# Fillers issued by another engine, a longer ring of pages, and other rules for the first pages in a two-layer graph network with experts

## The chip, the cores and the metric

The kernel runs on one core of one Trainium2 chip, all in float32 (bfloat16 only for exact small counts). The core has TensorE (PE: matrix products, with PEld for its weight loads), VectorE (DVE), ScalarE (ACT), GpSimd (POOL) and SyncE (SP, which here only issues transfers). The metric is the device time of one execution in microseconds; the median of three runs counts.

## The reference

8192 tokens (128 graphs of 64 nodes) of 256 values go through two layers. Each layer is a graph network followed by a mixture of experts:

```python
# layer 0
x = x + gnn0(layernorm(x), adj)        # adj @ x, 256 -> 1024, RMS norm, silu, 1024 -> 256
h = layernorm(x)
logits = h @ gate_w.T                  # 64 experts
top_logits, indices = top_k(logits, 6)
scores = softmax(top_logits)
y = sum over the six of scores[k] * (h @ lattice_weights[indices[k]])   # 256 x 256 each
x = x + layernorm(h + y @ out_w.T + out_b)
# layer 1
x = x + relu(adj @ ln(x) @ W_rel + ln(x) @ W_root)
x = x + sum over the best 2 of 8 experts of w[k] * (relu(f @ W1[e] + b1[e]) @ W2[e] + b2[e])   # f = layernorm(x)
```

The result depends on which experts each token chooses, so the kernel sorts tokens by expert while it runs.

## The kernel before

**Four stages.** (1) From 0 to about 584 us, 32 blocks of 256 tokens go through layer 0's graph network and its gate. For each token and each of its six experts POOL scatters a row of 258 values (256 values, the answer's place, the weight) with an indirect store into the table `r0x` in DRAM (`send`, L419, 12 stores of 128 rows per block). DVE keeps the books that give every row its place. (2) From 622 to 1097.6 us the experts work on *pages* of 128 rows. (3) From 1097.6 to about 1450 us layer 0's output and layer 1's graph network run, again 32 blocks; POOL scatters rows for layer 1's experts into `r1x`. (4) The rest is layer 1's experts, bound by PE's products.

**The expert stage.** Pages go in pairs. For each, SP loads two pages from `r0x` into a buffer `px` (`fetch(j)` in the kernel, `Router.fetch` at L652; 129 KB a page), PE transposes them (`flip`, L1159), ACT copies the transposes from PSUM to `pxT` (L1162), PE multiplies them by the experts' matrices, which all lie in SBUF (`apply`, L1188, eight products per pair), DVE scales the products by the weights back into `px` (L1192), and POOL scatters each page's rows to their tokens' places in `r0y` (`reply`, L426). `px` has 22 buffers of one pair each: the fetch of pair j + 22 waits until the replies of pair j have left its buffer. After 188 pairs of full or nearly full pages come 28 half pages (L649). Twelve *early* pages, one for each of the first twelve experts, are done ahead of the page table.

**Order of the work.** PE, DVE and ACT run in the order in which the kernel's loops issue their instructions (`staggered`: fetch stands twelve pairs ahead of apply, flip three). The order on SP and POOL is chosen by the framework's scheduler. A transfer issued by SP or ACT uses one of eight completion semaphores in turn, shared by both engines; it waits until the one before it on that semaphore is complete. POOL's transfers have eight of their own.

**Fillers.** The last page of an expert is not full. For each of the 64 experts a page of filler rows is stored behind its rows in `r0x` before any page that could read it: `fill_end(e)` reads four ends at a time into registers and issues the store (`fill`, L234). It is called in `apply(j)` for j below 64, on ACT's queue. Full pages have no filler rows; their fetches don't wait for the stores. ACT also loads six small vectors beside pairs 8 to 13 (`load_vectors`).

**Rounds and the first blocks.** The page table lists first up to R full pages of each expert (R is the number after the name `"r0"` in `Router(...)`), then the rest, then pages that are not full. The answers of the first R x 64 listed pages are told apart from the later ones (`"last"`, L432). In stage 3 `load_y(b)` loads the answers of block b; for b below READY it needs no later answer. `look_back`, called after block READY - 1, notes how far each expert's rows had come by then; if they don't fit the first pages, a slow branch waits for everything. `fold(b)`, from the eighth block on, adds two of the six answers on DVE before PE sums the others.

**Adjacency.** Each block of layers 0 and 1 uses one of four tiles (`load_adjacency`) of 128 x 2 x 128 values, of which only the diagonal 64 x 64 blocks are loaded; the rest was cleared once, at the start.

Of the kernel before, what the change touches and what calls it, by code (L numbers as in the profile page):

```python
# [19 lines left out]
P = 128  # L20
# [86 lines left out]
class Router:  # L107
# [502 lines left out]
                                       op0=ALU.add, op1=ALU.max)  # L610
        v.tensor_copy(self.total_pages, most)

    def fill_end(self, e):

        if e % 4 == 0:
            _, self.ends = self.nc.values_load_multi_w_load_instructions(
                self.last[0:1, e:e + 4], engines=[ENG.Activation], min_val=0, max_val=self.spare - self.pg,
                skip_runtime_bounds_check_because="the rows of an expert end in its chunk")
        self.fill(self.nc.scalar, self.ends[e % 4])

    def load(self, what, i, engine):

# [44 lines left out]
def two_layer_gnn_moe_kernel(ctx: ExitStack, tc: tile.TileContext, a: dict, out: bass.AP):  # L667
# [13 lines left out]
    K0 = 6  # L681
    E1, F1, _ = a["L1_ffn_W2"].shape
    EARLY = 12
    READY = 6
    FIRST = 4
    FOLD = 2
    LOOK = 20
# [49 lines left out]


    adjacency = []
    for i in range(4):  # L740
        at = const.tile([P, T, P], F32, name=f"at{i}")
        nc.gpsimd.memset(at, 0.0)
        adjacency.append(at)

    def load_adjacency(b):
        at = adjacency[b % 4]
        for g in range(2):
            nc.sync.dma_start(out=at[g * G:(g + 1) * G, :, g * G:(g + 1) * G],
                              in_=adjT[2 * b * T + g:2 * (b + 1) * T:2].rearrange("t m n -> m t n"))
        return at  # L750
# [24 lines left out]
    with tc.tile_pool(name="c0", bufs=1) as c0, \  # L775
            tc.tile_pool(name="work0", bufs=2) as work, \
            tc.tile_pool(name="ph0", bufs=4, space=PSUM) as ph_pool, \
            tc.tile_pool(name="ps0", bufs=2, space=PSUM) as psum, \
            tc.tile_pool(name="pm0", bufs=1, space=PSUM) as pmix:
        mean = c0.tile([P, P], F32, name="mean")  # L780
        nc.gpsimd.memset(mean, 1.0 / H0)
        route = pmix.tile([P, 2, T, E0], F32, name="route")
# [191 lines left out]
        aggregate(0)  # L974
        rest = lambda f: lambda b: f(b) if b else None

        r0 = Router(tc, const, small, dram, N, D, E0, K0, T, P, 14 * P, 4, "r0", 3, ((K0 * N // P - EARLY) // 4 * 4 + 4, E0 // 2 - 4), True)
        r1 = Router(tc, const, small, dram, N, D, E1, 2, T, 2 * P, N, 4, "r1", 1,
                    (N // P // 2 - E1 // 2, E1 // 4, E1 - 1), True, total=out, like=r0)
        assert W == r0.W  # L980
# [135 lines left out]
    with tc.tile_pool(name="wx0", bufs=3, reuse_waits="tile") as wx, \  # L1116
            tc.tile_pool(name="pt1", bufs=4, space=PSUM, reuse_waits="tile") as pt_pool, \
            tc.tile_pool(name="py1", bufs=4, space=PSUM, reuse_waits="tile") as py_pool:
        npair = (r0.pages + 1) // 2
        pairs = [dict(n=min(2, r0.pages - 2 * j), parts=1) for j in range(npair)]  # L1120
        pairs += [dict(n=2, parts=2) for j in range(E0 // 4)]
        regs = {}
        ring = [wx.tile([P, KD, C], F32, name="pxT", bufs=5)]
        over = dict(ln_g=r0.map.rearrange("p j e -> p (j e)")[:, :D], ln_b=r0.nth.rearrange("p j e -> p (j e)")[:, :D],
                    gamma=r0.end[:, :KD], beta=r0.delta[:, :KD], bg=r0.alloc[:, :E1], gbias=r0.none[:, :E1])

        def load_vectors(j):

            if 8 <= j < 14:
                name, v = (("ln_g", "L0_ffn_ln_g"), ("ln_b", "L0_ffn_ln_b"), ("gamma", "L1_gnn_ln_gamma"),  # L1130
                           ("beta", "L1_gnn_ln_beta"), ("bg", "L1_ffn_bg"), ("gbias", "L1_ffn_bias"))[j - 8]
                with nc.allow_non_contiguous_dma(reason="small vector"):
                    nc.scalar.dma_start(out=over[name], in_=a[v].rearrange("(c p) -> p c", p=P) if j in (10, 11)
                                        else rows_of(a[v]))
            if j == 18:
                nc.vector.tensor_add(over["bg"], over["bg"], over["gbias"])

        def fetch(j):
            Q = pairs[j]
            Q["px"] = px = wx.tile([P, 2, W], F32, name="px", bufs=22)  # L1140
            if j >= npair:
                regs["row"] = r0.load(2, 4 * (j - npair), ENG.SP)
                for i in range(4):
                    q, h = i // 2, i % 2 * P // 2
                    r0.fetch_rows(regs["row"][i], px[h:h + P // 2, q:q + 1, :], P // 2)
                return
            for q in range(Q["n"]):
                i = 2 * j + q
                if i % 4 == 0:
                    regs["row"] = r0.load(0, i, ENG.SP)  # L1150
                r0.fetch(i, regs["row"][i % 4], px[:, q:q + 1, :])

        def flip(j):
            Q = pairs[j]
            pt = pt_pool.tile([P, KD, C], F32, name="pt")
            n = Q["n"]
            for q in range(n):
                for k in range(KD):
                    nc.tensor.transpose(pt[:, k, ts(q, P)], Q["px"][:, q, ts(k, P)], ident)  # L1159
            if Q["parts"] == 1:  # L1160
                Q["xT"] = xT = ring.pop() if ring else wx.tile([P, KD, C], F32, name="pxT", bufs=5)
                nc.scalar.copy(xT[:, :, :n * P], pt[:, :, :n * P])  # L1162
                return
            Q["xT"] = []
            for q in range(n):
                xT = wx.tile([P, KD, C], F32, name="pxT", bufs=5)
                Q["xT"].append(xT)
                nc.vector.memset(xT[:, :, P // 2:P + P // 2], 0.0)
                for h in (0, 1):
                    nc.scalar.copy(xT[:, :, 3 * h * P // 2:3 * h * P // 2 + P // 2],  # L1170
                                   pt[:, :, q * P + h * P // 2:q * P + h * P // 2 + P // 2])

        def apply(j):
            Q = pairs[j]
            if j < E0:
                r0.fill_end(j)
            Q = pairs[j]
            if Q["parts"] == 2:
                regs["e"] = r0.load(3, 4 * (j - npair), ENG.PE)
            elif j % 2 == 0:  # L1180
                regs["e"] = r0.load(1, 2 * j, ENG.PE)
            py = py_pool.tile([P, 2, D], F32, name="py")
            px, xT, n, parts = Q["px"], Q["xT"], Q["n"], Q["parts"]
            for q in range(n):
                for h in range(parts):
                    e = regs["e"][2 * q + h if parts == 2 else (2 * j + q) % 4]
                    for k in range(KD):
                        nc.tensor.matmul(py[:, q, :], lhsT=xT[q][:, k, ts(h, P)] if parts == 2 else xT[:, k, ts(q, P)],  # L1188
                                         rhs=lat[:, ds(e, 1), k, :].rearrange("p o d -> p (o d)"),
                                         start=(h + k == 0), stop=(h == parts - 1 and k == KD - 1))  # L1190
            for q in range(n):
                nc.vector.tensor_scalar(px[:, q, :D], py[:, q, :], px[:, q, D + 1:D + 2], None, op0=ALU.mult)  # L1192
                r0.reply(2 * j + q, px[:, q, :], px[:, q, :D])


        stages = ((-12, fetch), (0, apply),
                  (-2, lambda j: flip(j) if j < 4 or j >= npair else None),
                  (-3, lambda j: flip(j) if 4 <= j < npair else None))

        def run(order, *more):  # L1200
            order = tuple(order)
            staggered(len(order), [*((lag, lambda n, f=f: f(order[n])) for lag, f in stages), *more])

        usual = r0.likely_pages // 2
        likely = (r0.likely_pages + E0 // 8) // 4 * 2
        ends = npair + r0.likely_halves // 4
        run((*range(usual), *range(npair, ends)), (0, load_vectors))
        wait = const.tile([1, 4], F32, name="wait")
        with tc.If(r0.needed(2 * usual)):
            run((*range(usual, likely), *range(ends, len(pairs))))  # L1210
            with tc.If(r0.needed(2 * likely)):
                run(range(likely, npair))

                nc.sync.dma_start(out=wait, in_=r0.answer[0:1, 0:4])
# [125 lines left out]
    with tc.tile_pool(name="c3", bufs=1, reuse_waits="tile") as c3, \  # L1340
# [5 lines left out]
        ln_g, ln_b, gamma, beta, bg = (over[x] for x in ("ln_g", "ln_b", "gamma", "beta", "bg"))  # L1346
        w_rel, w_root = (c3.tile([P, KD, D], F32, name="m_" + x) for x in ("rel", "root"))
        wg = load_matrix(c3, "L1_ffn_Wg")
        one = c3.tile([P, P], F32, name="one")
        nc.vector.memset(one, 1.0)  # L1350
        blocks = [dict() for _ in range(NB)]
# [2 lines left out]

        def load_y(b):
            B = blocks[b]
            B["y"] = y = work.tile([P, T, K0, D], F32, name="y", bufs=3)
            for t in range(T):
                d = nc.sync.dma_start(out=y[:, t],
                                      in_=r0.answer[ts(b * T + t, P * K0), :].rearrange("(p k) d -> p k d", k=K0))  # L1360
# [35 lines left out]
        def fold(b):  # L1396

            B = blocks[b]
            B["n"] = K0
            if b > READY + 1:  # L1400
                B["n"] = n = K0 - FOLD
                y = B["y"]
                nc.vector.tensor_add(y[:, :, :FOLD], y[:, :, :FOLD], y[:, :, n:])
# [266 lines left out]
    with tc.tile_pool(name="pt4", bufs=2, space=PSUM, reuse_waits="tile") as pt_pool, \  # L1670
# [7 lines left out]
        def finish(i):  # L1678
            if i >= 0:
                what, m, new = listed(i)  # L1680
                if i < E1:
                    r1.fill_end(i)
                if new and not (what == 0 and i % 2):
                    regs["e", what] = r1.load(what + 1, m, ENG.PE)
            share(i)
# [61 lines left out]
```

## Time and profile before

| | us |
|---|---|
| median of three runs | 1949.97 (1948.76 to 1953.71) |
| the profiled execution | 1948.88 |
| its span in the profile | 1947.1 |
| PE busy | 1845.0 (95%) |
| POOL busy | 1134.5 (58%) |
| PE busy in 584 to 622 | 22.05 of 38 |
| PE busy in 622 to 1097.6 | 451.47 of 475.6 |
| PE busy in 1097.6 to 1450 | 341.36 of 352.4 |
| PE busy in 1450 to 1947 | 479.27 of 497 |

The profile is of one execution. "L1188 PE MATMUL py<-lat,pxT" is a group of PE's instructions at line 1188 that write the tile `py` from `lat` and `pxT`. A wait is told as the waiting line, the line or transfer that released it, the sum in us, the number of times and the longest. "SPq" and "ACTq" are the issues of transfers on those engines' queues, which are not counted as busy time. Releasers are inferred: of several waits that end together only the last is named.

### The profile page before, as it was taken

How to read it: one execution, taken by the hardware profiler on the slowest of the kernel's cores; microseconds unless marked ns; L12 is line 12 of the kernel's file. 1: busy time of each engine (PE TensorE's matmuls, PEld its weight loads, DVE VectorE, ACT ScalarE, POOL GpSimd, SP SyncE). 2: the span in 40 equal slices, each digit the busy share in tenths (PEclk: the TensorE clock that was granted, in tenths of full speed). 3: DMA queues.
4: the chain of work that ended last, by engine and by line, in shares of the span. 5: the costliest groups of instructions: out<-in, count | busy, mean ns of one | idle time of the engine just before them, and what ended most of it. 6: DMA issues, size and time to landing. Idle time of an engine off the chain costs nothing. (4 is left out here: it accounts for less than half of the span.)

```text
span 1947.1 us, 35284 instructions
## 1 busy us (share of the span) xinstructions
PE 1845.0 (95%) x9906; PEld 1608.8 (83%) x9906; DVE 1146.9 (59%) x4256; ACT 1001.6 (51%) x2047; POOL 1134.5 (58%) x1114
## 2 busy tenths in 40 slices
PE   7999999999966898999999899999999999999996
PEld 6888888888844787888887788888888888888885
DVE  5899999999976333344433279999974222222221
ACT  5888898889841222222222156666663333333332
POOL 1377777777677677777777734444454544444443
PEclk9999999999977999999999999999999999999998
DMA  5134555544376988766666689878626766656653
GB/s 141 62 132 144 165 162 164 162 152 137 122 251 193 305 265 263 227 210 204 210 208 201 234 325 328 300 262 287 212 101 139 167 143 127 142 125 141 123 108 44
DMA packets 253085, 359.49 MB, mean 185 GB/s; under 512 B 53176, under 2 KB 210504, under 8 KB 252880
## 3 DMA queue, kind: packets, MB, share of 16 engines
q1 hardware_dynamic: 175904, 210.74, 36.9%
q0 software_dynamic: 62736, 135.21, 23.5%
q10 hardware_dynamic: 14240, 11.12, 1.8%
q8 instruction: 90, 1.47, 0.3%
q14 instruction: 115, 0.94, 0.2%
HBM read 193.27 MB, written 166.03 MB: 185 GB/s over the span
## 5 line engine op out<-in xcount | busy, mean ns | idle before, releaser
L419 POOL DMA_INDIRECT r0x<-xs,r0row x384 | 388.5, 1012 | 215.1 <-ACT lat L883 112.5
L426 POOL DMA_INDIRECT r0y<-px x390 | 378.7, 971 | 122.9 <-issue 40.0
L1188 PE MATMUL py<-lat,pxT 128*128 x1616 | 387.0, 384 | 20.8 <-ACT pxT L1162 17.6
L436 POOL DMA_INDIRECT out_x<-px x131 | 202.8, 1548 | 265.9 <-DVE px L1333 173.7
L1192 DVE TENSOR_SCALAR px<-py,px 128x256 f32<-128x256 f32 x390 | 170.8, 480 | 304.6 <-PE py L1188 298.4
L1188 PEld LDWEIGHTS py<-lat,pxT 128*128 128x128 f32 x1616 | 294.0, 192 | 61.2 <-ACT pxT L1162 23.9
L1162 ACT COPY pxT<-pt 128x512 f32<-128x512 f32 x188 | 109.7, 585 | 346.5 <-PE pt L1159 242.4
L1294 ACT ACTIVATE phid<-ph,pw 128x256 f32<-128x256 f32 (+1 forms) x264 | 122.0, 462 | 287.8 <-PE ph L1285 181.0
L419 POOL DMA_INDIRECT r1x<-xs,r1row x128 | 135.0, 1054 | 179.6 <-ACT hn L1447 55.9
L894 PE MATMUL ps<-lat 128*128 128x256 f32 x1024 | 238.9, 382 | 0.0
L858 PE MATMUL ph<-lat 128*128 128x256 f32 x1024 | 231.5, 385 | 3.2 <-DVE lat L881 2.0
L1310 PE MATMUL py<-fw,phid 128*128 (+1 forms) x1016 | 230.4, 380 | 0.0
L1285 PE MATMUL ph<-pxT,pw 128*128 128x256 f32 (+1 forms) x1056 | 227.3, 368 | 1.5 <-DVE px L1327 1.5
L858 PEld LDWEIGHTS ph<-lat 128*128 128x128 f32 x1024 | 195.0, 193 | 29.6 <-issue 2.7
L894 PEld LDWEIGHTS ps<-lat 128*128 128x128 f32 x1024 | 193.7, 192 | 27.8
L1285 PEld LDWEIGHTS ph<-pxT,pw 128*128 128x128 f32 x1056 | 193.2, 190 | 26.3 <-DVE px L1327 1.9
L1310 PEld LDWEIGHTS py<-fw,phid 128*128 128x128 f32 x1016 | 188.2, 190 | 22.5
L1321 DVE TENSOR_SCALAR p<-p 128x2 f32<-128x2 f32 (+1 forms) x69 | 12.6, 183 | 208.0 <-ACT p L1320 208.0
L1159 PE MATMUL pt<-ident,px 128*128 128x128 f32 x780 | 121.4, 276 | 7.0 <-DMA px<-r0x 6.7
L1327 DVE TENSOR_TENSOR px<-py,pb 128x512 f32<-128x512 f32 (+1 forms) x67 | 44.5, 664 | 138.3 <-PE py L1310 133.7
L881 DVE SCALAR_TENSOR_TENSOR lat<-ph,c_L_gnn_b,rms 128x256 f32<-128x256 f32 x256 | 111.9, 477 | 23.3 <-ACT rms L72 23.3
L1159 PEld LDWEIGHTS pt<-ident,px 128*128 128x128 f32 x780 | 97.5, 142 | 31.5 <-DMA px<-r0x 6.2
(337 smaller groups left out, 2959.6 us busy)
## 6 DMA issues: line engine op xcount, KB each, us to landing
y<-r0y SPq DMA_DIRECT2D x64, 768.0 KB
px<-r0x SPq DMA_DIRECT2D x376, 129.0 KB
pw<-in_L_ffn_W1b SPq DMA_DIRECT2D x41, 514.0 KB
x<-x SPq DMA_DIRECT2D x64, 256.0 KB
px<-r1x SPq DMA_DIRECT2D x28, 516.0 KB
r0x<-r0filler ACTq DMA_DIRECT2D x64, 129.0 KB
lat<-in_x SPq DMA_DIRECT2D x32, 256.0 KB
lat<-in_L_ffn_lattice_weights SPq DMA_DIRECT2D x8, 1024.0 KB
```

Source lines behind the costliest of these rows:

```text
L419: i = self.nc.gpsimd.indirect_dma_start(out=self.table[:, :], out_offset=bass.IndirectOffsetOnAxis(ap=row[:, t, k:k + 1], axis=0), in_=xs[ ...
L426: d = self.nc.gpsimd.indirect_dma_start(out=self.answer[:, :], out_offset=bass.IndirectOffsetOnAxis(ap=x[:, self.D:self.D + 1].bitcast(I32 ...
L436: i, d = f"{self.name}add{i}", self.nc.gpsimd.indirect_dma_start(out=self.total[:, :], out_offset=bass.IndirectOffsetOnAxis(ap=x[:, self.D ...
L858: nc.tensor.matmul(ph[:, c, :], lhsT=w1[:, k, ts(2 * j + c, P)], rhs=B["aggT"][:, k, :], start=(k == 0), stop=(k == KD - 1))
L881: nc.vector.scalar_tensor_tensor(hT[:, c, :], B["ph", c // 2][:, c % 2, :], b1[:, c:c + 1], B["rms"], op0=ALU.add, op1=ALU.mult)
L894: nc.tensor.matmul(B["po"][:, t, :], lhsT=B["hT"][:, c, ts(t, P)], rhs=w2[:, c, :], start=False, stop=(t == T - 1 and c == KH - 1))
L1159: nc.tensor.transpose(pt[:, k, ts(q, P)], Q["px"][:, q, ts(k, P)], ident)
L1188: nc.tensor.matmul(py[:, q, :], lhsT=xT[q][:, k, ts(h, P)] if parts == 2 else xT[:, k, ts(q, P)], rhs=lat[:, ds(e, 1), k, :].rearrange("p ...
L1192: nc.vector.tensor_scalar(px[:, q, :D], py[:, q, :], px[:, q, D + 1:D + 2], None, op0=ALU.mult)
L1285: nc.tensor.matmul(Q["up", c][:, :m], lhsT=Q["w"][:, k * F1 + c * P:k * F1 + (c + 1) * P], rhs=Q["xT"][:, k, :m], start=(k == 0), stop=(k ...
L1294: nc.scalar.activation(Q["hid"][:, c, :m], Q["up", c][:, :m], AF.Relu, bias=Q["w"][:, KD * F1 + c:KD * F1 + c + 1], scale=1.0)
L1310: nc.tensor.matmul(py[:, t, :], lhsT=Q["hid"][:, c, ts(t, P)], rhs=fw2[:, ds(e, 1), c, :].rearrange("p o d -> p (o d)"), start=(c == 0), s ...
```

## The change

Seven edits go together.

1. GpSimd's area for transfer descriptors (`dynamic_dma_scratch_size`) is 4096 bytes instead of the default 16384.
2. The adjacency tiles are made twice, in the pools of stage 1 (cleared by POOL) and of stage 3 (cleared by DVE), instead of once for the whole kernel.
3. `px` has 31 buffers instead of 22.
4. Layer 0's fillers are issued by SP, in `fetch(j)` for every second pair from 24 to 150, instead of by ACT.
5. R is 5 instead of 3.
6. READY is 12 instead of 6, with `look_back` after block 11; `fold` begins at block 8 as before (`WHOLE`).
7. `y` has four buffers instead of three.

```diff
-    def fill_end(self, e):
+    def fill_end(self, e, engine, issuer):
         if e % 4 == 0:
             _, self.ends = self.nc.values_load_multi_w_load_instructions(
-                self.last[0:1, e:e + 4], engines=[ENG.Activation], min_val=0, max_val=self.spare - self.pg,
+                self.last[0:1, e:e + 4], engines=[engine], min_val=0, max_val=self.spare - self.pg,
...
-        self.fill(self.nc.scalar, self.ends[e % 4])
+        self.fill(issuer, self.ends[e % 4])
...
-    READY = 6
+    READY = 12
+    WHOLE = 8
...
     adjacency = []
-    for i in range(4):
-        at = const.tile([P, T, P], F32, name=f"at{i}")
-        nc.gpsimd.memset(at, 0.0)
-        adjacency.append(at)
+
+    def clear_adjacency(pool, engine):
+        for i in range(4):
+            at = pool.tile([P, T, P], F32, name=f"at{i}")
+            engine.memset(at, 0.0)
+            adjacency.append(at)
 
     def load_adjacency(b):
-        at = adjacency[b % 4]
+        at = adjacency[b % 4 - 4]
...
+        clear_adjacency(c0, nc.gpsimd)
...
-        r0 = Router(tc, const, small, dram, N, D, E0, K0, T, P, 14 * P, 4, "r0", 3, ((K0 * N // P - EARLY) // 4 * 4 + 4, E0 // 2 - 4), True)
+        r0 = Router(tc, const, small, dram, N, D, E0, K0, T, P, 14 * P, 4, "r0", 5, ((K0 * N // P - EARLY) // 4 * 4 + 4, E0 // 2 - 4), True)
...
         def fetch(j):
             Q = pairs[j]
-            Q["px"] = px = wx.tile([P, 2, W], F32, name="px", bufs=22)
+            if j % 2 == 0 and 24 <= j < 24 + 2 * E0:
+                r0.fill_end((j - 24) // 2, ENG.SP, nc.sync)
+            Q["px"] = px = wx.tile([P, 2, W], F32, name="px", bufs=31)
...
         def apply(j):
-            Q = pairs[j]
-            if j < E0:
-                r0.fill_end(j)
             Q = pairs[j]
...
+        clear_adjacency(c3, nc.vector)
...
-            B["y"] = y = work.tile([P, T, K0, D], F32, name="y", bufs=3)
+            B["y"] = y = work.tile([P, T, K0, D], F32, name="y", bufs=4)
...
-            if b > READY + 1:
+            if b >= WHOLE:
...
-                    r1.fill_end(i)
+                    r1.fill_end(i, ENG.Activation, nc.scalar)
...
-    nc = bacc.Bacc("TRN2", target_bir_lowering=False, num_devices=1)
+    nc = bacc.Bacc("TRN2", target_bir_lowering=False, num_devices=1, dynamic_dma_scratch_size=4096)
```

In the built program the order on PE is the same. DVE has four more clears, at the start of stage 3, and `look_back` later. On SP three fillers stand after the early pages' fetches and ahead of the last lattice load, then come the fetches of 30 pairs, then one filler for two pairs and later one for each pair until all 64 are out. At the start of stage 3 SP's order is m_rel, m_root, two adjacency loads, four loads of y, x, two of y, and so on; before, it was two loads of y, m_rel, m_root, two of y, x. On POOL the last answer stands behind the branch that decides on the slow path.

## The prediction

> **What bounds the kernel now.** I read the page's busy shares first, then the sums by stage, then the waits of each stage that has idle time, then single instructions.
>
> ```profile
> PE 1845.0 (95%) x9906; PEld 1608.8 (83%) x9906; DVE 1146.9 (59%) x4256; ACT 1001.6 (51%) x2047; POOL 1134.5 (58%) x1114
> ```
>
> TensorE is idle for 1947.1 - 1845.0 = 102 us. Only a stage where it idles can give anything back. Sums over stretches of the expert stage (622 to 1097.6) and after it; the columns are the stretch, its length, busy time of PE, PEld, DVE, ACT and POOL, PE's clock, the DMA engines' busy share, GB/s:
>
> ```profile
> 640.00:700.00 60.00, 52.33 (x277) 44.08 (x276) 20.04 (x48) 13.46 (x23) 42.65 (x45) 1.00 0.96 293
> 800.00:900.00 100.00, 100.00 (x556) 88.36 (x555) 40.67 (x94) 27.00 (x47) 76.22 (x79) 1.00 0.69 209
> 1000.00:1066.00 66.00, 61.12 (x311) 49.31 (x310) 22.58 (x52) 15.21 (x26) 50.24 (x52) 1.00 0.67 206
> 1097.00:1126.00 29.00, 18.61 (x115) 15.88 (x114) 9.74 (x35) 6.08 (x12) 22.18 (x23) 0.88 0.97 368
> ```
>
> PE loses time at the stage's start, at the end of its full pages, and at layer 1's start; between, it is full. The waits of PE and ACT in 622 to 800, of SP in 622 to 1097, and of PE in 1097.6 to 1126.3 (engine, line, releaser: us in all, times, longest):
>
> ```profile
> PE py L1188 <- ACT pxT L1162: 17.6, 21, 2.0
> ACT pxT L1162 <- DMA px<-r0x: 73.4, 29, 5.4
> ```
>
> ```profile
> SPq L652 <- DMA r0y<-px: 164.9, 115, 3.8
> ```
>
> ```profile
> PE ps L1382 <- DMA y<-r0y: 10.4, 7, 5.6
> ```
>
> First pair: PE waits for ACT's copy of a pair (L1162), and ACT waits for a *page fetch* that its copy doesn't read (PE's flip had read it). In ACT's queue stand the filler stores (L234), and those share completion semaphores with SP's fetches, so a filler waits for a fetch well ahead of PE. SP's line: fetches wait for an answer to have left an old `px` buffer, and the answers come at POOL's pace:
>
> ```profile
> L234 ACTq DMA_DIRECT2D r0x<-r0filler x64: 338/339/379, 625.9 to 792.9; - x64
> L426 POOL DMA_INDIRECT r0y<-px x390: 967/969/1172, 630.2 to 1130.5; - x195
> ```
>
> ```profile
> 1006.58 0.97 POOL L426 DMA_INDIRECT r0y<-px  x1 [0.30 <-issue]
> 1007.86 0.97 POOL L426 DMA_INDIRECT r0y<-px  x1 [0.30 <-DMA r0y<-px]
> ...
> 1009.14 0.97 POOL L426 DMA_INDIRECT r0y<-px  x1 [0.30 <-DVE px L1192]
> ```
>
> An answer takes 0.97 us plus 0.30 us of issue: 1.275 us, 2.55 us for a pair of pages. PE's pace, eight products of L1188 per pair counted in the trace: pair 6 at 640.0 and pair 66 at 793.9 (2.565 per pair, POOL's pace, handed on through SP and the fillers in ACT's queue); pair 72 at 808.7 and pair 150 at 977.6 (2.165, its own); pair 162 at 1004.4 and pair 186 at 1065.8 (2.56, POOL's again, now through the ring of 22 `px` buffers). The ring in single instructions: the answers of pair 146 stand at 1006.58 and 1007.86 (above), pair 168 is fetched at 1011.51 and multiplied at 1020.58, 14.0 us after its ring predecessor's first answer; for pairs 174 and 186 it is 13.5 and 13.3.
>
> **What the Trainium skill says.** "Trainium Kernel Development and Optimization", Key Constraints: DMAs issued from SP, ACT and POOL run on the same 16 engines, and another issuer saves only issue time. The trace agrees that issue is small (0.34 us a filler); what moving it saves here is ACT's wait. "SBUF — State Buffer", SBUF size: 192, 224, or 256?: 16 KiB per partition is the scratch for GpSimd's descriptors, a ring. "DMA: Bandwidth & Descriptors", The descriptor swizzle: a GpSimd transfer to 128 partitions makes 9 read and 9 write descriptors per engine. Eight semaphores serve POOL's transfers in turn, so at most eight are under way: an estimate from that page is 72 of each kind per engine. No line of the trace shows POOL waiting for room in the ring.
>
> **The change part by part.**
>
> *Fillers on SP.* ACT loses 64 stores and 16 register loads, and with them the 17.6 us of PE's wait. SP issues them between fetches, 64 x about 0.5 us with its register moves = 32 us over 300 us, in a queue that now waits 164.9 us; the 8.3 MB are moved as before. Three go out near 602, before the last lattice load and the first fetch, whose wait (for the last scattered rows, until 619.4) covers them. ACT keeps six small loads beside pairs 8 to 13, which share semaphores with fetches of pairs 20 to 28. At the 1.43 us per pair of before's first fetches those land at about 652 to 664, so PE is held to about pair 16 at 665 rather than 660: 5 us, which costs nothing below 11 us (next part).
>
> *31 pairs.* The last pairs are still tied to POOL: pair k is multiplied no earlier than 13.5 us after pair k-31's first answer. POOL's answers start at 630.2 as before (before that it sends rows back to back until 614.55, then 12 early answers). So pair 187 starts at 630.2 + 156 x 2.55 + 13.5 = 1041.5, if POOL runs without gaps. PE's own pace gives 630.2 + 187 x 2.167 = 1035.4: the ring decides, by 6 us (11 without the 5 us above). Before, pair 187 started at about 1068.4, with three gaps in POOL's answers (at 664.6, 668.4 and 675.6, together 3.9 us) that came from PE being late. Gain: 9 x 2.55 = 23.0 us for sure if the gaps stay, 27 if they vanish; I take 25. The 28 half pages (29 us, PE busy 30.5 of 31) follow as before: PE ends the stage at about 1072.5 instead of 1097.6.
>
> *Layer 1's start.* Adjacency tiles: the early loads under stage 1 go away, and four DVE clears (128x256 floats; the nearest row, a scale of that size on L1192, is 0.48 us) and their loads stand at the start. SP's order was y, y, m_rel, m_root, y, y, x; now m_rel, m_root, two adjacency loads, four y. By the issues in the trace (0.42 and 1.23 us, about 0.4 for each adjacency load, gaps) y starts 2.7 us later; 0.6 MB ahead of it at 368 GB/s is up to 1.6 us more, less what m_root no longer takes later. PE's wait of 10.4 us grows by 3; bounds 0 and 8. The clears lie beside PE's wait for y (DVE busy 9.7 of 29 us); without that cover 1.9 us.
>
> *Rounds 5, READY 12.* Page counts and products are the same, in another order. Before, block 6's y waited for all answers (its load went out at 1137.1, harmlessly). With PE 22 us earlier and POOL ending at much the same time, block 6 would be due near 1115, and the old rule would cost some 20 us. Now block 12 is the first to wait; at 10.3 us per block it is due near 1200, its buffer free near 1160, and all answers have landed by about 1140. Nothing. The slow branch for odd routings stays untaken: from the inputs, no expert gets more rows in the first 12 blocks than its first pages hold (the closest has 36 to spare). The fourth y buffer only lets loads start earlier.
>
> *POOL's tail.* Layer 1's first send to `r1x` was at 1155.1, POOL free at 1137; it moves to about 1133, while POOL is free between 1133 and 1140. 0 to 7 us late, and four `xs` buffers hide it: nothing.
>
> *Descriptor area.* Not shown in the trace. Below: 0, since nothing waits for the ring. Above: room for one transfer at a time would make each of 402 answers last as long as its landing, some 5 us, a disaster. I take 0, since 72 of a ring that held far more is little.
>
> Sum: -25 + 3 = -22. Against the profiled execution of 1948.88 (span 1947.1 and 1.8 around it): 1926.9. The median is 1.1 above that execution: **1928.0**.
>
> **The rivals.** (A) *The gain becomes a wait for y.* From 1073 to 1131 answers (0.132 MB per 1.275 us = 104 GB/s) run beside layer 1, whose loads need 1.9 MB per 10.3 us (y 1.57, x 0.26, adjacency 0.07) = 185 GB/s. For it: PE waits for y now at 0.97 DMA share. Against: 289 is under the 368 GB/s seen there. If y came 20% late over the 25 us that are new, and the start cost 8: gain 25 - 13 = 12, so 1938. (B) *The smaller descriptor area slows POOL* (slower than before). POOL's 402 answers are one unbroken chain that sets the end of the stage; from 22/402 = 0.055 us more per answer nothing is left; at 0.1 us it is +40 - 22, 1968. The 384 sends of layer 0, back to back at their end, would add to it. For it: the area shrinks to a quarter. Against: at most eight transfers under way. (C) *More than forecast*: gaps gone, start free: -27, 1923. (D) *The ring isn't what holds the end*: fillers interleaved in SP's queue delay fetches as they delayed ACT; then 3 to 5 us remain, about the same time.
>
> **How the numbers follow.** Chances: forecast 0.62 (1924 to 1934), A 0.15 (1934 to 1944), C 0.11 (1918 to 1924), B 0.08, D 0.04. The range leaves out B, D and the far part of C: 1920 to 1945. A change of 0.3%, 5.8 us, is about what can be told from none: faster is forecast, A and C, 0.88; same 0.04; slower 0.08.
>
> **What would show it.** PE's wait for ACT in 622 to 800 nearly gone, pair 66 near 770; pairs after about 170 at 2.55 us with `px<-r0x` waits left; PE's last expert product near 1072; then a wait of about 13 us for y; block 12's y not waited for; answers still 1.275 us apart. Wrong if answers are further apart, if PE waits long for y between 1080 and 1140, or if SP's fetches wait for fillers.

## The result, and the profile after

| | before | changed |
|---|---|---|
| median | 1949.25 us (1948.24 to 1953.71, six runs) | 1933.59 us (1932.56 to 1934.47, six runs) |
| ratio, with its 95% interval | | 0.9916 (0.9904 to 0.9929) |
| the profiled execution / its span | 1948.88 / 1947.1 us | 1934.47 / 1932.7 us |

The changed kernel is 15.7 us faster by the medians, 14.4 us by the spans. The forecast was 1928.0 us, 22 us faster, with a range of 1920 to 1945. The sign and the range hold, but in part by luck: two large terms that the forecast put at nothing have opposite signs and partly cancel.

The busy shares of the changed kernel, from the page:

```profile
PE 1832.8 (95%) x9906; PEld 1608.0 (83%) x9906; DVE 1149.1 (59%) x4260; ACT 1002.0 (52%) x2047; POOL 1137.2 (59%) x1114
```

The same stretches of work as shown before: the start and the steady part of the expert stage, its last full pages, and layer 1's first 29 us; then one stretch that has no counterpart before. Columns are the stretch, its length, busy time of PE, PEld, DVE, ACT and POOL, PE's clock, the DMA engines' busy share, GB/s:

```profile
640.00:700.00 60.00, 57.70 (x319) 50.61 (x318) 23.71 (x55) 15.51 (x27) 45.67 (x48) 1.00 0.94 288
800.00:900.00 100.00, 100.00 (x556) 88.36 (x555) 40.33 (x92) 26.92 (x46) 75.95 (x79) 1.00 0.74 225
972.00:1038.00 66.00, 61.80 (x324) 51.40 (x323) 23.66 (x54) 15.80 (x27) 50.14 (x53) 1.00 0.66 206
1069.60:1098.60 29.00, 14.48 (x93) 12.35 (x91) 7.97 (x29) 4.49 (x9) 22.29 (x23) 0.82 0.96 346
1119.00:1131.00 12.00, 1.36 (x9) 0.91 (x7) 3.71 (x12) 0.00 (x0) 5.70 (x6) 0.72 0.76 247
```

The first line shows the repair at the stage's start: PE is busy for 57.7 of 60 us instead of 52.3. The third shows that the last pages are still short of work. In the fourth PE has less than before (14.5 us instead of 18.6). The last is new: of the 12 us from 1119 PE works 1.4, DVE 3.7 and ACT none. PE's waits over the whole run, four of interest:

```profile
PE ps L1386 <- DMA y<-r0y: 16.3, 6, 10.3
PE pg L1530 <- ACT xn3T L1524: 11.8, 2, 11.5
...
PE pt L1165 <- DMA px<-r0x: 6.2, 7, 2.8
...
PE py L1191 <- ACT pxT L1168: 2.3, 2, 1.5
```

PE's wait for ACT's copies is 2.3 us instead of 17.6. The first wait for y is 10.3 us instead of 5.6. The second line is the stall after 1119: PE waits for ACT's copy into `xn3T`, the transposed input of layer 1's gate. ACT and POOL in order of time around it:

```profile
1117.69 0.48 ACT L36 ACTIVATE std<-bn_mv,eps 128x2 f32<-128x2 f32 x2
1131.18 0.58 ACT L1524 COPY xn3T<-ps 128x512 f32<-128x512 f32 x1 [13.01 <-DMA r0y<-px]
```

```profile
1125.25 0.97 POOL L426 DMA_INDIRECT r0y<-px  x1 [0.30 <-issue]
1131.82 0.97 POOL L426 DMA_INDIRECT r0y<-px  x1 [5.59 <-DMA r0y<-px]
```

ACT's copy of block 0 waits 13.0 us, and the named releaser is an *answer* of the expert stage, which the copy doesn't use. It starts just after POOL has passed the branch for odd routings: POOL waits there for its transfers to land, and then raises their semaphores by what the branch not taken would have added (0.34 us from 1130.54). The copy's waits stand in ACT's queue as instructions of their own, and one of the seven takes nearly all the time:

```profile
L1524 ACTq EVENT_SEMAPHORE  x7: 38/38/13390, 1117.3 to 1131.1; - x7
```

It runs from 1117.45 to 1130.84 and waits for two semaphores, one of SP's and ACT's transfers, complete since 1126.4, and one of POOL's. On the latter the last answer had landed by 1122.8; the trace's next update of it is at 1130.81, within POOL's raise. So no answer's landing released the copy; the raise did. The built program agrees: the copy wants four of POOL's semaphores at 1600 or 1616, and the answers ahead of the branch bring them to 1568 only.

The reason is memory. `xn3T` lies on memory of `px` buffers that the branch would use. It has the same place in both kernels (from byte 169664 of a partition), but with 31 buffers `px` begins at 164832, before at 179808. Before the change the copy waited for PE alone.

The stall costs more than its wait. The first products after it, and the same work in the kernel before (shown first):

```profile
1143.11 1.03 PE L1526 MATMUL pg<-m_L_ffn_Wg,xn3T 128*128 128x8 f32 x8
1144.00 2.82 PE L1382 MATMUL ps<-ident,y 128*128 128x128 f32 x24
```

```profile
1131.82 1.88 PE L1530 MATMUL pg<-m_L_ffn_Wg,xn3T 128*128 128x8 f32 x8 [11.46 <-ACT xn3T L1524]
1133.55 4.90 PE L1386 MATMUL ps<-ident,y 128*128 128x128 f32 x24
```

They take 2.9 us longer. From 1131.8 to 1138.3 the granted clock was 0.54; in the kernel before it was 1.00 from 1143.1 to 1147.0. So PE loses 11.5 us by waiting and 2.9 by slower products.

Last, the end of the program. Drains and the update of POOL's semaphores are no busy time; they are listed under the last lines of each kernel, before first, then changed (engine queue, operation, count: shortest/median/longest in ns, first and last start):

```profile
L1743 POOLq DRAIN  x3: 46/107/6237, 1940.0 to 1946.8; - x3
```

```profile
L1713 POOLq INC_SWDGE_SEM  x1: 1675/1675/1675, 1938.3 to 1938.3; - x1
```

```profile
L1747 POOLq DRAIN  x3: 46/107/1092, 1930.8 to 1932.4; - x3
```

```profile
L1717 POOLq INC_SWDGE_SEM  x1: 412/412/412, 1930.3 to 1930.3; - x1
```

POOL's longest drain falls from 6.24 to 1.09 us and the update from 1.68 to 0.41: 6.4 us at the very end, where no work lies beside it.

So the 14.4 us of the spans, by PE's milestones in both traces (times in us from the span's start):

| milestone | before | changed | changed earlier by |
|---|---|---|---|
| pair 0's first product | 625.2 | 623.3 | 1.9 |
| pair 60 | 778.1 | 757.8 | 20.3 |
| pair 150 | 977.6 | 952.8 | 24.8 |
| pair 187, the last full pair | 1068.0 | 1040.2 | 27.8 |
| last product of the expert stage ends | 1097.6 | 1070.2 | 27.4 |
| block 0's last four products of layer 1's graph network begin (L1492 / L1496) | 1132.3 | 1109.4 | 22.9 |
| block 1's | 1142.2 | 1119.3 | 22.9 |
| block 2's | 1153.3 | 1144.9 | 8.4 |
| last block's | 1449.5 | 1441.4 | 8.1 |
| PE's last L1285 / L1288 product ends | 1927.6 | 1919.4 | 8.2 |
| end | 1947.1 | 1932.7 | 14.4 |

The gain of 27.4 loses 4.5 at layer 1's start and 14.5 between its blocks 1 and 2 (11.5 + 2.9 above), and the end gives 6.2 back.

### The profile page after: what moved, and what is told of

Read it like the earlier page. It is cut to its first block, busy times and chain, and to the rows that moved or that the text cites. A ratio compares the mean times of both kernels' runs of the same rounds, so it can differ in the third digit from the quotient of the medians.

```text
span 1932.7 us, 35276 instructions
## 1 busy us (share of the span) xinstructions
PE 1832.8 (95%) x9906; PEld 1608.0 (83%) x9906; DVE 1149.1 (59%) x4260; ACT 1002.0 (52%) x2047; POOL 1137.2 (59%) x1114
## 5 line engine op out<-in xcount | busy, mean ns | idle before, releaser
L1288 PE MATMUL ph<-pxT,pw 128*128 128x256 f32 (+1 forms) x1056 | 227.3, 369 | 1.5 <-DVE px L1330 1.5
L1288 PEld LDWEIGHTS ph<-pxT,pw 128*128 128x128 f32 x1056 | 193.3, 191 | 26.1 <-DVE px L1330 1.9
L885 DVE SCALAR_TENSOR_TENSOR lat<-ph,c_L_gnn_b,rms 128x256 f32<-128x256 f32 x256 | 111.9, 477 | 22.9 <-ACT rms L72 22.8
```

Of the source, the lines that this page charges most:

```text
L885: nc.vector.scalar_tensor_tensor(hT[:, c, :], B["ph", c // 2][:, c % 2, :], b1[:, c:c + 1], B["rms"], op0=ALU.add, op1=ALU.mult)
L1288: nc.tensor.matmul(Q["up", c][:, :m], lhsT=Q["w"][:, k * F1 + c * P:k * F1 + (c + 1) * P], rhs=Q["xT"][:, k, :m], start=(k == 0), stop=(k ...
```

## The experiments

One set of four runs (`y3`, `b_4k`, `b_fillsp`, `after_fillact`) and the last run (`after_nobranch`) fell on chips on which TensorE's mean clock was 0.93 and the kernel before took 2273 and 2280 us; there PE reaches layer 1 so late that the waits in question can't show, and differences under 1% mean little. Experiments 1 to 7 ran where the clock was 0.98 and the kernel before took 1949 us; they carry the verdicts. Times of pairs and blocks are read from one profiled execution of each kernel.

**1. Three y buffers instead of four: is the wait before xn3T one for memory?**

```diff
-            B["y"] = y = work.tile([P, T, K0, D], F32, name="y", bufs=4)
+            B["y"] = y = work.tile([P, T, K0, D], F32, name="y", bufs=3)
```

> The changed kernel with three y buffers instead of four, a second time, because TensorE's clock was irregular (0.93) for every kernel of the first set. Theory (memory): ACT's wait of 11.5 us before xn3T, until POOL has passed the slow branch, is gone; PE's waits for y stay near 16 us; 10 to 14 us under the changed kernel, some 26 us under the kernel before, ratio near 0.986. Rival (answers): PE stands there anyhow for y; within 3 us of the changed kernel, ratio 0.990 or more.

Measured: 1916.50 us, ratio 0.9836 (0.9823 to 0.9850), 17.1 us under the changed kernel (15.1 by the spans) and 32.5 under the kernel before. That is more than the 10 to 14 expected, which counted the wait without the slower products after it. ACT in order of time in this kernel:

```profile
1117.35 0.48 ACT L36 ACTIVATE std<-bn_mv,eps 128x2 f32<-128x2 f32 x2
1119.19 0.58 ACT L1524 COPY xn3T<-ps 128x512 f32<-128x512 f32 x1 [1.36 <-PE ps L89]
```

The copy waits 1.4 us, for PE, and starts at 1119.19 instead of 1131.18. The last products of blocks 0 to 3 begin at 1109.0, 1119.0, 1130.0 and 1141.1, where the changed kernel had a step of 25.6 us from block 1 to 2. PE waits for y as long as before the edit:

```profile
PE ps L1386 <- DMA y<-r0y: 15.5, 5, 10.8
```

The memory theory holds and the rival falls: neither the last answers nor the loads of y held PE there. In the built program `xn3T` now begins at byte 157376, and the copy waits for PE alone. POOL passes the branch as late as in the changed kernel (1130.7), so it is the place of `xn3T` that matters. The fourth buffer cost 15 us, given the 31 `px` buffers, and brought nothing that shows. This kernel is also the better version: experiments 4 to 7 and their diffs are measured against it.

**2. The descriptor area alone.**

```diff
-    nc = bacc.Bacc("TRN2", target_bir_lowering=False, num_devices=1)
+    nc = bacc.Bacc("TRN2", target_bir_lowering=False, num_devices=1, dynamic_dma_scratch_size=4096)
```

> The kernel before with the descriptor area of 4096 bytes alone, a second time. Theory (area is cleaned at the end): POOL's last drain and the semaphore update before it give 6.4 us, ratio 0.9967. Rival (ring too small): ratio above 1.01. Rival (nothing): 0.9995 to 1.0005.

Measured: 1939.03 us, ratio 0.9949 (0.9936 to 0.9963), 10.0 us less. The drain on POOL in this kernel, otherwise the kernel before:

```profile
L1743 POOLq DRAIN  x3: 46/107/1092, 1936.8 to 1938.5; - x3
```

```profile
L1713 POOLq INC_SWDGE_SEM  x1: 412/412/412, 1936.4 to 1936.4; - x1
```

From PE's last L1285 product to the end it takes 13.1 us instead of 19.5: the 6.4 us of the theory, with this one edit. What the drain does in that time isn't shown. Answers stay 1.28 us apart (median), so the rival of a ring too small falls. The rest is not explained: pair 0 starts at 622.6 instead of 625.2 because the scattering of layer 0's rows ends at 609.8 instead of 613.6. With the small area that end was 610.4 to 613.2 in the other profiles, with the large one 613.1 and 613.6, so a real effect of 2 us on layer 0 is possible and not shown.

**3. Fillers on SP alone, 22 buffers.**

```diff
         def fetch(j):
             Q = pairs[j]
+            if j % 2 == 0 and 24 <= j < 24 + 2 * E0:
+                r0.fill_end((j - 24) // 2, ENG.SP, nc.sync)
             Q["px"] = px = wx.tile([P, 2, W], F32, name="px", bufs=22)
...
         def apply(j):
             Q = pairs[j]
-            if j < E0:
-                r0.fill_end(j)
```

> The kernel before with the fillers issued by SP and 22 px buffers, a second time. Theory (ring): only the gaps in POOL's answers are saved, 3 to 5 us, ratio 0.9975 to 0.9985; PE's wait for ACT goes, its waits for px grow from 6.7 to some 20 us. Rival (fillers): 15 us less or more, ratio 0.992 or below.

Measured: 1946.22 us, ratio 0.9987 (0.9980 to 0.9993): 2.8 us less. (The new arguments of `fill_end` come with the edit.) Pair 60 comes at 759.7, 18 us earlier than before, pair 150 at 970.9 and pair 187 at 1064.4, only 3.6 us earlier; POOL's answers have no gap over 1.5 us. PE's largest sum of waits is now the one for `px`, 6.7 us before:

```profile
PE pt L1161 <- DMA px<-r0x: 13.6, 20, 2.8
```

The ring theory holds: PE runs ahead and is caught by POOL's 2.55 us per pair. Only the gaps are saved.

**4. Fillers on ACT, 31 buffers.**

```diff
         def fetch(j):
-            if j % 2 == 0 and 24 <= j < 24 + 2 * E0:
-                r0.fill_end((j - 24) // 2, ENG.SP, nc.sync)
...
         def apply(j):
+            if j < E0:
+                r0.fill_end(j, ENG.Activation, nc.scalar)
```

> The changed kernel with three y buffers and the fillers on ACT. Without the wait before xn3T nothing hides a later end of the expert stage. Theory (ring): 0 to 7 us slower than the same kernel with fillers on SP, PE's wait for ACT between 5 and 18 us. Rival (fillers): 15 us slower or more.

Measured: 1931.77 us, ratio 0.9913 (0.9899 to 0.9926), 15.3 us slower than the kernel of experiment 1 (12.4 by the spans). PE's wait for ACT in 620 to 800 is back:

```profile
PE py L1191 <- ACT pxT L1166: 17.2, 15, 2.9
```

Pair 60 comes at 779.8, 20.8 us later than in experiment 1, pair 187 at 1054.4, 14.6 us later. From pair 150 to 187 it takes 2.15 us per pair, PE's own pace: with 31 buffers and this late start the ring no longer binds at all. The ring hid only 20.8 - 14.6 = 6 us. My expectation of 0 to 7 us was wrong; the rival number came true. Against the kernel before, pair 187 comes 3.6 us earlier with the fillers alone, 13.6 with the buffers and the other edits but without the fillers' move (1068.0 - 1054.4), and 28.2 with both (1039.8). Counted from pair 0, whose start differs by up to 4 us between these profiles, it is 4, 10 and 27. Each edit removes one of two limits of the same stage, and either alone leaves the other.

**5. READY 6 and three rounds.**

```diff
-    READY = 12
+    READY = 6
...
-"r0", 5, (
+"r0", 3, (
```

> The changed kernel with three y buffers, and with READY 6 and three rounds as before. The forecast put some 20 us on the old rule. Theory (loads run ahead): block 6's y can't be loaded before the last answer, now issued after the slow branch at 1132, has landed near 1137; PE wants it near 1141 to 1146 in the kernel with three buffers, so 0 to 6 us slower than that kernel (ratio 0.9836 to 0.987). Rival (as forecast): 15 to 20 us slower, ratio 0.991 or more.

Measured: 1924.05 us, ratio 0.9871 (0.9856 to 0.9886), 7.5 us slower than experiment 1. SP's wait between 1105 and 1135, and PE in order of time:

```profile
SPq L1363 <- DMA r0y<-px: 19.4, 1, 19.4
```

```profile
1129.31 1.06 PE L1530 MATMUL pg<-m_L_ffn_Wg,xn3T 128*128 128x8 f32 x8
1133.91 2.79 PE L1386 MATMUL ps<-ident,y 128*128 128x128 f32 x12 [3.54 <-DMA y<-r0y]
```

Block 6's load waits 19.4 us on SP, until the last answer has landed (issued at 1129.31 instead of 1111.39), but PE loses only some 7: block 3 comes 17.9 us after block 2 instead of 11.1. PE waits 3.7 us for y there, and the 24 products on y then take 5.6 us instead of 2.8; the granted clock was 0.50 from 1133.9 to 1139.6. The rest of SP's wait is covered by y loaded ahead. So this edit is worth 7 us once PE is early (5.2 by the spans), near my upper bound of 6 and far from 20.

**6. Adjacency tiles in one place, 28 buffers.**

```diff
-    def clear_adjacency(pool, engine):
-        for i in range(4):
-            at = pool.tile([P, T, P], F32, name=f"at{i}")
-            engine.memset(at, 0.0)
-            adjacency.append(at)
+    for i in range(4):
+        at = const.tile([P, T, P], F32, name=f"at{i}")
+        nc.gpsimd.memset(at, 0.0)
+        adjacency.append(at)
...
-        clear_adjacency(c0, nc.gpsimd)
...
-            Q["px"] = px = wx.tile([P, 2, W], F32, name="px", bufs=31)
+            Q["px"] = px = wx.tile([P, 2, W], F32, name="px", bufs=28)
...
-        clear_adjacency(c3, nc.vector)
```

> The changed kernel with three y buffers, the adjacency tiles in one place for the whole kernel, cleared once, and 28 px buffers to make room. Theory: three pairs fewer put the end of the expert stage 3 x 2.55 = 7.7 us later (near 1077.5), and the loads of y stand first again, so PE's first wait for y falls from 10.8 to about 5.6 us: 2 to 4 us slower in sum, ratio 0.985. Rival (the clears and loads cost nothing, the DMA engines do): the wait stays near 10 us, 7 us slower, ratio 0.987. Rival (the ring doesn't hold the end): end of the stage within 2 us of 1069.8.

Measured: 1924.01 us, ratio 0.9870 (0.9855 to 0.9885), 7.5 us slower than experiment 1. In the trace both terms are as in the theory. Pair 187 stands at 1045.4 (1039.8 in experiment 1, with pair 0 at 622.0 instead of 624.0: 7.6 us later by that measure, for 3 x 2.55). And SP's order at layer 1's start is y first again:

```profile
1075.85 0.84 SPq L1360 DMA_DIRECT2D y<-r0y  x2
1076.73 0.43 SPq L1368 DMA_DIRECT2D m_rel<-in_L_gnn_W_rel  x1
```

```profile
1081.32 1.09 PE L1383 MATMUL ps<-ident,y 128*128 128x128 f32 x4 [5.59 <-DMA y<-r0y]
```

The first wait for y is 5.6 us instead of 10.8, and from the last expert product to block 0's last products it takes 35.8 us instead of 39.2. The expected sum was 2 to 4 us; the profiled execution, the fastest of its kernel, is 2.4 us longer in span than that of experiment 1, the medians differ by 7.5. The terms are shown, the sum is less certain.

**7. 32 buffers and an area of 2048 bytes.**

```diff
-name="px", bufs=31
+name="px", bufs=32
...
-dynamic_dma_scratch_size=4096
+dynamic_dma_scratch_size=2048
```

> The changed kernel with three y buffers, 32 px buffers and a descriptor area of 2048 bytes. Theory (ring): pair 187 2.55 us earlier, near 1037.3. Theory (area is cleaned at the end, in proportion to its size: 6.24 us for 16 KB, 1.09 for 4 KB): the last drain takes 0.2 to 0.6 us. Together 3 us under the kernel with three y buffers, ratio near 0.982. Rival (ring of descriptors too small): answers and sends more than 1.275 us apart, slower by 10 us or more.

Measured: 1915.94 us, ratio 0.9834 (0.9821 to 0.9847). Pair 187 stands at 1035.6; answers are 1.275 us apart. The drain:

```profile
L1747 POOLq DRAIN  x3: 46/107/928, 1910.7 to 1912.2; - x3
```

From 16 to 4 KB it fell by 5.15 us, from 4 to 2 KB by 0.16: it is not in proportion to the size. The median is 0.6 us under experiment 1, which can't be told from none (5.2 by the spans); the 3 us expected don't show in the medians. It has the lowest median measured here.

**8. The runs at the lower clock.** What was expected of the first set:

> The changed kernel with three y buffers instead of four; all else as changed. Theory (memory): the fourth y buffer, 12 KB a partition, pushes xn3T, xs and r1hot of layer 1 onto memory that px buffers of the slow branch use, so ACT's first copy to xn3T waits until POOL has passed that branch (1130.5 us); with three buffers that wait of 11.5 us is gone, PE's waits for y stay near 16 us, and the time is 1919 to 1924. Rival (answers): PE would stand there anyhow, because the last answers and the loads of y share the DMA engines until 1132; then y waits grow to some 25 us and the time is 1930 or more.

> The kernel before with GpSimd's descriptor area of 4096 bytes and nothing else. Theory (area is cleaned at the end): the last drain on POOL falls from 6.2 to about 1.1 us and the semaphore update ahead of it from 1.7 to 0.4; the time falls by 6.4 us to about 1943, answers stay 1.275 us apart. Rival (ring too small): answers further apart, 0.055 us each or more, the time rises by 20 us or more. Rival (nothing): within 1 us of before.

> The kernel before with the fillers issued by SP at the places of the change, 22 px buffers. Theory (ring): the last pairs are tied to POOL's answers through 22 buffers, so PE's gain at the start is given back at the end; only the gaps in POOL's answers, 3.9 us, are saved: 3 to 5 us less, PE's waits for px above 15 us. Rival (fillers): the 17.6 us of PE's wait for ACT are what the change saves: 15 us less or more.

> The changed kernel with the fillers on ACT as before, beside pairs 0 to 63. Theory (ring): 31 buffers alone carry most of the gain; PE may lose 5 to 18 us to ACT at the start, of which 11 fit under the ring's tie to POOL: 0 to 7 us slower than changed. Rival (fillers): without SP's issue the gain of the expert stage is gone, 15 us slower or more, near 1949.

Measured, as ratios to the kernel before in the same set: 0.9995 (0.9972 to 1.0019), 0.9983 (0.9962 to 1.0005), 0.9977 (0.9952 to 1.0002) and 0.9989 (0.9960 to 1.0019). None tells the theories apart. The last drain was 1.10 us with 4096 bytes and 6.24 with 16384 there too. The last run left out the branch for odd routings, with all four y buffers:

```diff
-        with tc.If(r0.needed(2 * usual)):
-            run((*range(usual, likely), *range(ends, len(pairs))))
...
```

> The changed kernel, four y buffers and all, with the slow branch for odd routings left out (these inputs don't take it, so the work done is the same; other routings would need it). Theory (memory of the branch): xn3T still lies on memory of px buffers, but now waits only for answers up to the 357th of 402, sent near 1070; the 11.5 us wait is gone, layer 1's blocks start 11 us apart, and the time is within 3 us of the kernel with three y buffers, ratio 0.982 to 0.985. Rival (four buffers of y delay it in another way: more loads ahead, DMA engines full): the wait before the third block stays, ratio 0.990 or more.

Measured: 2270.64 us, ratio 0.9963 (0.9937 to 0.9988). PE ended the expert stage at 1427.9 and POOL its answers at 1430.4, and `xn3T` was wanted only at 1469, so there was nothing left to wait for, and the time says nothing of either theory. That it is the branch, and not the last answers of the pages in use, which the copy waits for stands on the semaphore's updates in the changed kernel's trace and on the built program; by a run of its own it isn't shown.

## Why the prediction was right or wrong, point by point

**Fillers on SP: right.** PE's wait for ACT fell to 2.3 us (5 forecast), pair 66 stood at 770.8 (770 forecast). Among SP's waits none of a fetch is for a filler. Experiments 3 and 4 show what the forecast did not say: the move is worth 3 us with 22 buffers and 15 with 31 (12 by the spans).

**31 pairs: right, a little small.** Pair 187 was forecast at 1041.5 and stood at 1040.2 (before at 1068.0, which the prediction has as about 1068.4); the end of the stage at 1072.5 and it was 1070.2. The step as written (13.5 us after pair k-31's first answer, two answers per 2.55 us) held: for pair 187 it was 12.9, and 12.7 and 11.9 in experiments 6 and 7. POOL's three gaps vanished, so the upper end of 23 to 27 applied.

**Layer 1's start: right in kind, 3 forecast, 4.5 measured.** Within its bounds of 0 and 8. SP issued y 3.7 us after PE's end (0.15 before), where 2.7 later was forecast. Experiment 6 shows that with the tiles cleared once most of this goes away.

**"The fourth y buffer only lets loads start earlier": wrong, the step that failed.** The same holds for "POOL's tail ... nothing", which asked only when POOL's sends would be late. The prediction asked what the buffer does for the loads and not where it puts the tiles behind it: those lie on memory that the 31 `px` buffers had taken, and ACT came to wait for POOL's branch. The measured price is 14.5 us in the trace and 17.1 in the medians of experiment 1. It was to be had from the built program, in which ACT's first copy to `xn3T` has new waits for POOL's transfers; the prediction doesn't mention them. Before the change ACT made this copy at 1142.5 and POOL was past the branch by 1137.0, so a wait there would have cost nothing; with PE 22.9 us earlier it costs 14.5 of them.

**"Descriptor area ... I take 0": wrong, 6.4 us too little.** I asked only whether the ring could run full. Nothing shows that it did: answers stayed as far apart with 4096 and with 2048 bytes. The estimate of 72 descriptors stays untested: the page it rests on counts them for one transfer of 1 MiB, no run here shows the count for an indirect store of 128 rows, and what the ring holds isn't given. What the prediction left out is that the program ends by draining POOL, for longer with the larger area; in the trace of before this is the 6.24 us ahead of the end. The lower bound was 0, so the forecast left no room for a gain here.

**READY: right that it costs nothing; "some 20 us" for the old rule is wrong.** With three y buffers it is 7 (experiment 5). SP's wait was 19.4 us; the forecast took such a wait for PE's.

**The rivals.** A gave 1938 by y arriving late for long; a loss of that size came at that place, but through memory and POOL's branch. B, slower answers, fell in every run. C's premise, no gaps, came true. D fell: fetches didn't wait for fillers, and PE's waits for `px` at the end are the ring's.

In sum: forecast -25 + 3 = -22; measured by the spans -27.4 + 4.5 + 14.5 - 6.2 = -14.6, with 0.2 lost among rounding and small waits. That the forecast was near is partly luck: +14.5 and -6.2 were not in it and partly cancel, and -27.4 was 2.4 better than taken.

## What to carry to other kernels

A buffer added in one stage, or a longer ring in the stage before it, changes which tiles share memory. Here a tile that came to lie on memory of a stage that wasn't finished waited for it, a branch not taken included: list the waits of the next stage's first instructions in the built program before and after, and price each new one at the time when the engine will arrive, not when it arrived before. Price a stall of PE with the products after it. Two limits on the same stage (here a queue that holds up copies, and a ring tied to a slower engine) have to be lifted together; each alone gave less than half (by pair 187, counted from pair 0, 4 and 10 us of 27). Read the tail of the trace too: here what stood after the last product had no cover.

## What the runs showed of the hardware that was not expected

POOL's last drain depends on the size of GpSimd's descriptor area: 6.24 us with 16384 bytes, 1.09 to 1.10 with 4096, 0.93 with 2048. The update of POOL's semaphores depends on it too: with 16384 bytes 1.06 us at the branch and 1.68 at the end, with 4096 bytes 0.34 to 0.36 and 0.41 to 0.43, with 2048 bytes 0.34 and 0.37. Answers of 128 rows stayed 1.275 to 1.277 us apart (medians) with all three sizes.

After PE's wait of 11.5 us in the changed kernel the granted clock was 0.54 for the next 6.5 us, and 32 products took 2.9 us longer than the same ones before. After a wait of 3.5 us in experiment 5 it was 0.50 over the next 5.7 us, and 24 products took 2.8 us longer than in experiment 1.
